# A graph layer's message sums: 128 single rows and 24 gathered chunks per block in place of 96 and 28, with row offsets computed on VectorE

## The chip, the core and the metric

The kernel runs on one core of a Trainium2 chip. The metric is the device time of one launch in microseconds. Before the change, three runs took 15717.78, 15709.04 and 15708.98 us, a median of 15709.04.

In the profile PE is TensorE, DVE VectorE, ACT ScalarE, POOL GpSimd and SP SyncE. ACT and SP can issue DMAs too; their queues are written ACTq and SPq. L234 is line 234 of the kernel.

## The reference, cut to what matters

There are 50,000 nodes with 128 features and 1,650,000 edges, sorted by destination. Each edge has one of two types.

```python
Xs = X[src]
m_data = Xs @ W_data.T + b_data
m_ctrl = Xs @ W_control.T + b_control
msg = jnp.where((edge_types == 0)[:, None], m_data, m_ctrl)
agg = jax.ops.segment_sum(msg, dst, num_segments=X.shape[0])
h = x + jax.nn.relu(agg + (X @ W_self.T + b_self))
out = (h - mean(h)) / sqrt(var(h) + 1e-5)      # over the 128 features
```

So the row `X[src]` has to be fetched for every edge, and rows are summed by destination and type. The weights can be applied to the sums instead of to every edge.

## The kernel before

**Blocks and chunks.** The edges are cut into blocks of `BE = C * CH + X` = 28 * 128 + 96 = 3680 edges; there are 449 blocks, and ten of them (`GB`) make a group. A block has 28 chunks of 128 edges and one more "chunk" of 96. A block's work goes in `Q` = 4 steps of `R` = 7 chunks; the 96 extra edges belong to the fourth step.

**Two ways to fetch rows.** The rows of a 128-edge chunk come with one indirect DMA issued by POOL (L246), which reads 128 node numbers from a tile and gathers 128 rows of 512 bytes into a tile `y`. `y` has 70 buffers. The rows of the 96 extra edges come one by one, into the tile `yx`: SP and ACT issue 48 plain DMAs of 512 bytes each (L234). For that, the engine loads 12 node numbers into registers with one instruction (L229), once per step, which I call a turn; the DMA's address is the register times the row's length.

**Sums.** DVE makes a one-hot matrix per chunk (L198), which tells for each edge its destination within a window of `W` = 36 nodes and its type. PE multiplies the fetched rows with it (L249), so a step's sums by destination and type stand in PSUM (`acc`, four buffers). DVE counts edges by destination (L208, L213), and PE spreads the counts over rows (L252). DVE then adds a step's `acc` to the block's sums (`add`, L260) at a place that it loads into a register.

**Windows.** A block's destinations lie in a window of `B` = 128 nodes; sums run in a ring of three tiles. ACT copies the part of the last block's sums that the next window shares (`take_over`, L263 and L265). PE applies the weights (`layer`, L270 to L273), DVE makes h and its moments (L278 to L282), ACT takes the root (L284), DVE scales (`store`, L290 and L292), and SP stores the block (L293). SP also loads the windows of x and of its transpose (L187, L189).

**Order.** The order of the instructions on each engine is written out by hand, by the loop at the end of `straight`. In iteration b there stand, in this order: the windows of block b + 3; in every tenth iteration the loads of the next group's edges (`load_edges`, L95 and L99, in SP's queue); the last `add` of block b - 1 and the `take_over`; then for each step q the products of block b, with `layer`, `add`, `moments`, the one-hot of block b + 2, `store` and `counts` among them, and a turn of single rows for block b + 2 on SP and on ACT. On ACT a block is thus: copy, root, four turns of rows. On SP it is: two window loads, a turn of rows, a store, three turns of rows.

Of the kernel before, what the change touches and what calls it, by code (L numbers as in the profile page):

```python
# [11 lines left out]
F32 = mybir.dt.float32  # L12
BF16 = mybir.dt.bfloat16
I32 = mybir.dt.int32
AF = mybir.ActivationFunctionType
ALU = mybir.AluOpType
AX = mybir.AxisListType
# [3 lines left out]

N = 50000
D = 128
E = 1650000
P = 128
EPS = 1e-5
# [2 lines left out]
DST_PAD = 65536  # L29


R = 7
W = 36
Q = 4
B = 128
C = R * Q
X = 96
C1 = C + 1
BE = C * CH + X
NBLK = -(-E // BE)  # L40
REST = E - (NBLK - 1) * BE
RCH = -(-REST // CH)
LAST = REST - (RCH - 1) * CH
assert RCH <= C
GB = 10
# [5 lines left out]
U = 35  # L51
CPP = -(-(-(-E // CH) + U) // P)
NCH = CPP * P
# [11 lines left out]
def row_bcast(ap, n=P):  # L65
    return bass.AP(tensor=ap.tensor, offset=ap.offset, ap=[[0, n], *ap.ap])


def straight(ctx, tc, c, x, x_t, src_t, dst_t, etype_t, src_x, dst_first, out):
# [10 lines left out]
    nc = tc.nc  # L80
    keep = ctx.enter_context(tc.tile_pool(name="keep", bufs=1))
    keep_ps = ctx.enter_context(tc.tile_pool(name="keep_ps", bufs=1, space=bass.MemoryType.PSUM))
    eds = ctx.enter_context(tc.tile_pool(name="eds", bufs=2))
# [3 lines left out]
    ps = ctx.enter_context(tc.tile_pool(name="ps", bufs=4, space=bass.MemoryType.PSUM))  # L87
    ps_o = ctx.enter_context(tc.tile_pool(name="ps_o", bufs=2, space=bass.MemoryType.PSUM))

    idx_g, d_g, t_g, one_g, col_g = {}, {}, {}, {}, {}  # L90
    stats = keep.tile([P, 2, GROUPS], F32, name="stats")

    def load_edges(g):
        t = eds.tile([1, GB * X], I32, name="one_g")
        nc.sync.dma_start(t, src_x[None, g * GB * X:(g + 1) * GB * X])  # L95
        one_g[g] = t
        for name, a, of in (("idx_g", src_t, idx_g), ("d_g", dst_t, d_g), ("t_g", etype_t, t_g)):
            t = eds.tile([P, GC], I32, name=name)
            nc.sync.dma_start(t, a[:, g * GC:(g + 1) * GC])  # L99
            of[g] = t  # L100


    load_edges(0)
    BL = TBL
    first_i = keep.tile([P, BL, Q], I32, name="first_i")
    nc.sync.dma_start(first_i.rearrange("p b q -> p (b q)"), row_bcast(dst_first))
    base = keep.tile([P, BL, 1], F32, name="base")
    nc.vector.tensor_scalar(base, first_i[:, :, 0:1], 0.0, float(N - B), op0=ALU.max, op1=ALU.min)
    nc.vector.memset(base[:, 0:1, :], 0.0)
    nc.vector.memset(base[:, NBLK - 1:, :], float(N - B))  # L110
    begin = keep.tile([P, BL, Q], F32, name="begin")
    nc.vector.tensor_tensor(begin, first_i, base.to_broadcast([P, BL, Q]), op=ALU.subtract)
    nc.vector.tensor_scalar(begin, begin, 0.0, float(B - W), op0=ALU.max, op1=ALU.min)
    place_i = keep.tile([1, BL, Q], I32, name="place_i")
    nc.vector.tensor_copy(place_i, begin[0:1, :, :])
    nc.vector.tensor_tensor(begin, begin, base.to_broadcast([P, BL, Q]), op=ALU.add)
    base_i = keep.tile([1, BL], I32, name="base_i")
    nc.vector.tensor_copy(base_i, base[0:1, :, 0])
    shift = keep.tile([1, NBLK], F32, name="shift")
    nc.vector.memset(shift, 0.0)  # L120
    nc.vector.tensor_tensor(shift[:, 1:], base[0:1, 1:NBLK, 0], base[0:1, :NBLK - 1, 0], op=ALU.subtract)
    shift_i = keep.tile([1, NBLK], I32, name="shift_i")
    nc.vector.tensor_scalar(shift_i, shift, 0.0, float(B), op0=ALU.max, op1=ALU.min)


    num = keep.tile([P, 2 * W], F32, name="num")
    nc.gpsimd.iota(num, pattern=[[1, 2 * W]], base=0, channel_multiplier=0,
                   allow_small_or_imprecise_dtypes=True)
    num_ps = keep_ps.tile([P, 2 * W], F32, name="num_ps")
    nc.vector.tensor_copy(num_ps, num)  # L130
# [3 lines left out]
    for t in range(2):  # L134
        nc.vector.memset(to_row[:, t, t:t + 1], 1.0)
    bias = keep.tile([3, D], F32, name="bias")
    for i, b in enumerate((c["b_data"], c["b_ctrl"], c["b_self"])):
# [4 lines left out]
    RING = 3  # L142
    sums = [keep.tile([P, 3, 2 * B], F32, name=f"sums{i}") for i in range(RING)]
    for t in sums:
# [4 lines left out]
    def columns(g):  # L149
# [4 lines left out]
        rel_b, d_b = (a.rearrange("p (b c) -> p b c", c=C1) for a in (rel, d))  # L154
        nc.vector.tensor_tensor(rel_b[:, :, :C].rearrange("p b (q r) -> p b q r", r=R),
                                d_b[:, :, :C].rearrange("p b (q r) -> p b q r", r=R),
                                first[:, :, :, None].to_broadcast([P, GB, Q, R]), op=ALU.subtract)
        nc.vector.tensor_tensor(rel_b[:, :, C:], d_b[:, :, C:], first[:, :, Q - 1:], op=ALU.subtract)
        col = eds.tile([P, GC], F32, name="col_g")
        nc.vector.tensor_scalar(col, t, 0.0, float(W), op0=ALU.not_equal, op1=ALU.mult)  # L160
        nc.vector.tensor_tensor(col, col, rel, op=ALU.add)
        chk = eds.tile([P, GC], F32, name="chk")
        nc.vector.scalar_tensor_tensor(chk, d, float(DST_PAD), rel, op0=ALU.is_lt, op1=ALU.mult)
        nc.vector.tensor_reduce(stats[:, 0, g:g + 1], chk, AX.X, ALU.min)
        nc.vector.tensor_reduce(stats[:, 1, g:g + 1], chk, AX.X, ALU.max)
        col_g[g] = col

    def chunks_of(b, q):

        n = C1 if b < NBLK - 1 else RCH if b < NBLK else 0  # L170
        return range(q * R, max(q * R, min((q + 1) * R if q < Q - 1 else C1, n)))

    def steps_of(b):
        return [q for q in range(Q) if len(chunks_of(b, q))]
# [3 lines left out]
    ohs, cnts, ys, accs, xws, xTs, pos, hs, mvs, sds = {}, {}, {}, {}, {}, {}, {}, {}, {}, {}  # L178

    def base_of(b):  # L180
        return nc.values_load(base_i[0:1, b:b + 1], engines=[SP], min_val=0, max_val=N - B,
                              skip_runtime_bounds_check_because="it was clamped to this")

    def window(b):
        at = base_of(b)
        xw = stp.tile([B, D], F32, name="xw", bufs=5)
        nc.sync.dma_start(xw, x[bass.ds(at, B), :])  # L187
# [4 lines left out]
    def onehot(b):  # L192
# [3 lines left out]
        n = C1 if b < NBLK - 1 else RCH  # L196
        oh = ohp.tile([P, C1, 2 * W], F32, name="oh")
        nc.vector.tensor_tensor(oh[:, :n, :], col_g[g][:, i * C1:i * C1 + n, None].to_broadcast([P, n, 2 * W]),  # L198
# [3 lines left out]
    def counts(b):  # L202

        cnt = ohp.tile([P, Q, 2 * W], BF16, name="cnt")
        with nc.allow_low_precision(reason="whole numbers up to R + 1"):
            whole = [q for q in range(Q) if len(chunks_of(b, q)) == R]
            n = len(whole)
            nc.vector.tensor_reduce(cnt[:, :n, :], ohs[b][:, :n * R, :].rearrange("p (q r) w -> p q w r", r=R),  # L208
                                    AX.X, ALU.add)
            for q in steps_of(b):  # L210
# [5 lines left out]

    SHARE = X // 2
    TURN = SHARE // Q
    RANGE = dict(min_val=0, max_val=N - 1, skip_runtime_bounds_check_because="a node's number")

    def single_rows(b, q):

        if q == 0:
            ys[b] = stp.tile([X, D], F32, name="yx", bufs=AHEAD + 2)
        g, i = divmod(b, GB)
        both = []
        for j, (eng, dma) in enumerate(((SP, nc.sync), (ACT, nc.scalar))):
            at = j * SHARE + q * TURN
            _, nodes = nc.values_load_multi_w_load_instructions(  # L229
                one_g[g][0:1, i * X + at:i * X + at + TURN], engines=[eng], **RANGE)  # L230
            both.append([(dma, at + k, node) for k, node in enumerate(nodes)])
        for pair in zip(*both):
            for dma, row, node in pair:
                dma.dma_start(ys[b][row:row + 1, :], x[bass.ds(node, 1), :])  # L234

    def products(b, q):
        g, i = divmod(b, GB)
# [2 lines left out]
        for k in ks:  # L240
            if k == C:
                r, y = X, ys.pop(b)
            else:
                r = LAST if b == NBLK - 1 and k == RCH - 1 else P
                y = gat.tile([P, D], F32, name="y")
                nc.gpsimd.indirect_dma_start(  # L246
# [20 lines left out]
    def layer(b):  # L267
        a = sums[b % RING]
        po = ps_o.tile([B, D], F32, name="po")
        nc.tensor.matmul(po, xTs.pop(b), c["wselfT"], start=True, stop=False)  # L270
        nc.tensor.matmul(po, a[0:3, 2, :B], bias, start=False, stop=False)  # L271
        for t in range(2):
            nc.tensor.matmul(po, a[:, t, :B], c["wmsgT"][:, t * D:(t + 1) * D], start=False, stop=t == 1)  # L273
        pos[b] = po

    def moments(b):
# [6 lines left out]
        sd = stp.tile([B, 1], F32, name="sd")  # L283
        nc.scalar.activation(sd, mv[:, 1:2], AF.Sqrt, bias=c["eps"][:B, :])  # L284
        hs[b], mvs[b], sds[b] = h, mv, sd
# [9 lines left out]
    with tc.manual_schedule():  # L295
# [5 lines left out]
        for b in range(AHEAD):  # L301
            for q in range(Q):
                single_rows(b, q)
        for b in range(NBLK + 1):
            if b + 3 < NBLK:
                window(b + 3)
            g, i = divmod(b, GB)
# [41 lines left out]
    both = keep.tile([2, 1], F32, name="both")  # L349
# [9 lines left out]
def general(ctx, tc, c, x, src, dst, etype, out):  # L359
# [166 lines left out]
    with tc.For_i(0, BGROUPS, 1) as g:  # L526
# [43 lines left out]
        sd = grp.tile([NB, G], F32, name="sd")  # L570
        nc.scalar.activation(sd, mv[:, :, 1], AF.Sqrt, bias=eps[:NB, :])
        rstd = grp.tile([NB, G], F32, name="rstd")
# [8 lines left out]
def gnn_resnorm(  # L581
# [46 lines left out]
    with ExitStack() as own:  # L628
        straight(own, tc, c, x, x_t, src_t, dst_t, etype_t, src_x, dst_first, out)
# [38 lines left out]
```

## Time and profile before

| what | value |
|---|---|
| median of the runs | 15709.04 us |
| the profiled execution's own time | 15709.39 us |
| its span in the profile | 15707.6 us |
| busy: PE, DVE, ACT, POOL | 62%, 24%, 2%, 76% |
| granted TensorE clock | 1.00 |
| DMA queue of POOL: packets, MB | 401760, 823.58 |
| DMA queue of SP (q1): packets, MB | 256650, 120.61 |
| DMA queue of ACT (q10): packets, MB | 43446, 11.29 |

The busy share counts what an engine computes. Register steps, waits and the issuing of DMAs aren't in it, so an engine that issues DMAs all the time can stand there as idle. A group's line gives its count, its busy time, the mean of one, and behind the second bar the idle time before it with who ended most of it. In a timeline each line is a start, a length, the engine (with q for its queue), the source line, the operation and how many were merged. In a line's own view the three numbers in the middle are the shortest, median and longest duration in ns, and then come the first and the last start in the window.

All 40 slices of the span look alike: the kernel is one steady loop of 449 blocks, some 35 us each.

### The profile page before, as it was taken

What the parts mean: (1) busy time and instruction counts of PE and PEld (TensorE: products, weight loads), DVE (VectorE), ACT (ScalarE), POOL (GpSimd) and SP (SyncE); (2) the same over time, 40 slices, a digit from 0 to 9 for tenths busy, and PEclk for the clock granted to TensorE, in tenths of its full rate; (3) what the DMA queues carried; (4) which work ended last, traced back from release to release, by engine and by line L of the source; (5) the groups of instructions that cost most, each with busy time, mean ns of one, the idle gap of its engine ahead of it and who ended that gap; (6) DMA issues with size and microseconds to landing.
All of it is one profiled execution on the core that took longest, in us unless ns stands there. A gap on an engine that the chain in (4) does not pass through costs nothing.

```text
span 15707.6 us, 248219 instructions
## 1 busy us (share of the span) xinstructions
PE 9719.2 (62%) x33193; PEld 7477.1 (48%) x33194; DVE 3846.6 (24%) x5740; ACT 365.0 (2%) x903; POOL 11860.3 (76%) x12563
## 2 busy tenths in 40 slices
PE   5666666666666666666666666666666666666666
PEld 4444444444444444444444444444444444444444
DVE  3222222222222222222222222222222222222222
ACT  0000000000000000000000000000000000000000
POOL 7777777777777777777777777777777777777777
DMA  2222222222222222222222222222222222222222
GB/s 65 62 62 62 62 63 62 62 62 62 62 62 62 63 62 62 62 62 62 62 62 63 62 62 62 62 62 62 62 63 62 62 62 62 62 62 62 63 62 58
DMA packets 703530, 971.47 MB, mean 62 GB/s; under 512 B 267712, under 2 KB 500803, under 8 KB 701856
## 3 DMA queue, kind: packets, MB, share of 16 engines
q0 software_dynamic: 401760, 823.58, 20.1%
q1 hardware_dynamic: 256650, 120.61, 2.9%
q10 hardware_dynamic: 43446, 11.29, 0.3%
q14 instruction: 1397, 11.44, 0.2%
q8 instruction: 277, 4.54, 0.1%
HBM read 924.99 MB, written 29.43 MB: 61 GB/s over the span
## 4 chain that ended last, share of the span: by engine, by line
DMA 39%; issue 37%; PE 14%; POOL 8%; ACTq 2%; DVE 0%; SPq 0%; POOLq 0%; ACT 0%; DVEq 0%
DMA y<-in_x,idx_g 38%; PE acc L249 9%; POOL y L246 8%; PE po L273 2%; PE po L271 1%; DMA yx<-in_x 1%; PE po L270 1%; ACTq L234 1%; ACTq L229 0%; PE acc L252 0%; SPq L234 0%; POOLq L246 0%; SPq L229 0%; DVE sums L260 0%; DVE st L280 0%
## 5 line engine op out<-in xcount | busy, mean ns | idle before, releaser
L246 POOL DMA_INDIRECT y<-in_x,idx_g x12555 | 11859.4, 945 | 3832.3 <-issue 2666.4
L249 PE MATMUL acc<-oh,y 128*128 128x72 f32 x25110 | 8397.3, 448 | 5957.2 <-DMA y<-in_x,idx_g 5852.6
L249 PEld LDWEIGHTS acc<-oh,y 128*128 128x128 f32 x25110 | 6240.9, 314 | 7996.6 <-DMA y<-in_x,idx_g 7247.8
L260 DVE TENSOR_TENSOR sums<-acc,sums 128x108 f32 x1794 | 486.0, 271 | 10835.0 <-PE acc L252 9773.4
L208 DVE TENSOR_REDUCE cnt<-oh 128x216 bf16<-128x1512 f32 (+1 forms) x449 | 1268.5, 2825 | 0.1
L198 DVE TENSOR_TENSOR oh<-col_g,num_ps 128x2088 f32<-128x2088 f32 (+1 forms) x449 | 1030.7, 2296 | 0.0
L252 PEld LDWEIGHTS <-to_row 128*128 128x128 bf16 x3588 | 654.4, 198 | 0.0
L273 PE MATMUL po<-wmsgT,sums 128*128 128x128 f32 x1796 | 548.7, 461 | 0.0
L213 DVE TENSOR_REDUCE cnt<-oh 128x72 bf16<-128x576 f32 (+1 forms) x449 | 526.1, 1172 | 0.0
L265 ACT COPY sums<-sums 128x384 f32 x448 | 229.4, 512 | 11662.5 <-DMA yx<-in_x 11590.1
L252 PE MATMUL acc<-cnt,to_row 128*128 128x36 bf16 x3588 | 480.1, 217 | 0.0
L273 PEld LDWEIGHTS po<-wmsgT,sums 128*128 128x128 f32 x1796 | 416.3, 322 | 100.7 <-issue 100.7
L278 DVE SCALAR_TENSOR_TENSOR h<-po,xw 128x128 f32<-128x128 f32 x449 | 130.8, 291 | 949.2 <-PE po L273 949.2
L271 PE MATMUL po<-bias,sums 3*128 3x128 f32 x898 | 355.6, 497 | 9.5 <-DVE sums L260 8.2
L270 PE MATMUL po<-wselfT,xT 128*128 128x128 f32 x898 | 348.7, 492 | 0.0
L249 PE MATMUL acc<-oh,yx 96*128 96x72 f32 x896 | 284.6, 421 | 7.6 <-DMA yx<-in_x 7.6
L271 PEld LDWEIGHTS po<-bias,sums 3*128 3x128 f32 x898 | 223.3, 308 | 110.1 <-issue 110.1
L249 PEld LDWEIGHTS acc<-oh,yx 96*128 96x128 f32 x896 | 235.6, 323 | 7.8 <-DMA yx<-in_x 7.8
L270 PEld LDWEIGHTS po<-wselfT,xT 128*128 128x128 f32 x898 | 228.9, 317 | 0.0
L284 ACT ACTIVATE sd<-mv,eps 128x1 f32<-128x1 f32 x449 | 132.2, 295 | 3667.7 <-DVE mv L282 3667.7
L292 DVE TENSOR_SCALAR o<-h,mv,rstd 128x128 f32<-128x128 f32 x449 | 155.9, 347 | 16.6
L280 DVE BATCH_NORM_STATS2 st<-h 128x6 f32<-128x128 f32 x449 | 132.3, 295 | 15.3
(61 smaller groups left out, 294.9 us busy)
## 6 DMA issues: line engine op xcount, KB each, us to landing
yx<-in_x ACTq DMA_DIRECT2D x21504, 0.5 KB
yx<-in_x SPq DMA_DIRECT2D x21504, 0.5 KB
y<-in_x,idx_g POOLq DMA_INDIRECT x12555
xw<-in_x SPq DMA_DIRECT2D x449, 64.0 KB
xT<-in_x_t SPq DMA_DIRECT2D x449, 64.0 KB
out<-o SPq DMA_DIRECT2D x449, 64.0 KB
idx_g<-in_src_t SPq DMA_DIRECT2D x45, 145.0 KB
d_g<-in_dst_t SPq DMA_DIRECT2D x45, 145.0 KB
```

Of the source, the lines that this page charges most:

```text
L198: nc.vector.tensor_tensor(oh[:, :n, :], col_g[g][:, i * C1:i * C1 + n, None].to_broadcast([P, n, 2 * W]), num_ps[:, None, :].to_broadcast( ...
L208: nc.vector.tensor_reduce(cnt[:, :n, :], ohs[b][:, :n * R, :].rearrange("p (q r) w -> p q w r", r=R), AX.X, ALU.add)
L213: nc.vector.tensor_reduce(cnt[:, q, :], ohs[b][:, k[0]:k[-1] + 1, :].rearrange("p r w -> p w r"), AX.X, ALU.add)
L234: dma.dma_start(ys[b][row:row + 1, :], x[bass.ds(node, 1), :])
L246: nc.gpsimd.indirect_dma_start(out=y[:r], out_offset=None, in_=x, in_offset=bass.IndirectOffsetOnAxis(ap=idx_g[g][:r, i * C1 + k:i * C1 + ...
L249: nc.tensor.matmul(acc[:, :2, :].rearrange("p t w -> p (t w)"), y[:r], ohs[b][:r, k, :], start=k == ks[0], stop=k == ks[-1])
L252: nc.tensor.matmul(acc[:, 2, :], to_row[:, t, :], cnts[b][:, q, t * W:(t + 1) * W], start=t == 0, stop=t == 1)
L260: nc.vector.tensor_tensor(part, accs.pop((b, q)), part, op=ALU.add)
L265: nc.scalar.copy(sums[b % RING][:, :, :B], sums[(b - 1) % RING][:, :, bass.ds(at, B)])
L270: nc.tensor.matmul(po, xTs.pop(b), c["wselfT"], start=True, stop=False)
L271: nc.tensor.matmul(po, a[0:3, 2, :B], bias, start=False, stop=False)
L273: nc.tensor.matmul(po, a[:, t, :B], c["wmsgT"][:, t * D:(t + 1) * D], start=False, stop=t == 1)
```

## The change

A block becomes 24 chunks and 128 single edges: `R` goes from 7 to 6, `X` from 96 to 128, `BE` from 3680 to 3200, and the number of blocks from 449 to 516. The windows shrink with it: `W` from 36 to 34, `B` from 128 to 112. A turn is 16 rows per queue instead of 12.

The registers hold byte offsets instead of node numbers. After a group's node numbers are loaded, DVE multiplies them all by the 512 bytes of a row (a tile `at_g` of one partition); SP and ACT load their registers from that tile. x and the target tile are viewed as bytes, so that the address of a row is the register itself.

```diff
+U8 = mybir.dt.uint8
...
+ROW = 4 * D
...
-R = 7
-W = 36
+R = 6
+W = 34
 Q = 4
-B = 128
+B = 112
 C = R * Q
-X = 96
+X = 128
...
-    idx_g, d_g, t_g, one_g, col_g = {}, {}, {}, {}, {}
+    idx_g, d_g, t_g, at_g, col_g = {}, {}, {}, {}, {}
...
     def load_edges(g):
         t = eds.tile([1, GB * X], I32, name="one_g")
         nc.sync.dma_start(t, src_x[None, g * GB * X:(g + 1) * GB * X])
-        one_g[g] = t
+        at = eds.tile([1, GB * X], I32, name="at_g")
+        nc.vector.tensor_scalar(at, t, float(ROW), None, op0=ALU.mult)
+        at_g[g] = at
...
-    RANGE = dict(min_val=0, max_val=N - 1, skip_runtime_bounds_check_because="a node's number")
+    RANGE = dict(min_val=0, max_val=(N - 1) * ROW, skip_runtime_bounds_check_because="where a node's row is")
+    x_bytes = x.rearrange("n d -> (n d)").bitcast(U8)[None, :]
...
-            _, nodes = nc.values_load_multi_w_load_instructions(
-                one_g[g][0:1, i * X + at:i * X + at + TURN], engines=[eng], **RANGE)
-            both.append([(dma, at + k, node) for k, node in enumerate(nodes)])
+            _, rows = nc.values_load_multi_w_load_instructions(
+                at_g[g][0:1, i * X + at:i * X + at + TURN], engines=[eng], **RANGE)
+            both.append([(dma, at + k, row) for k, row in enumerate(rows)])
         for pair in zip(*both):
-            for dma, row, node in pair:
-                dma.dma_start(ys[b][row:row + 1, :], x[bass.ds(node, 1), :])
+            for dma, k, row in pair:
+                dma.dma_start(ys[b][k:k + 1, :].bitcast(U8), x_bytes[:, bass.ds(row, ROW)])
```

## The prediction

> **What bounds the kernel now.** I read the page first, then the timelines of POOL, ACT and SP over one block, then the row line L234 by itself.
>
> ```profile
> span 15707.6 us, 248219 instructions
> ...
> L246 POOL DMA_INDIRECT y<-in_x,idx_g x12555 | 11859.4, 945 | 3832.3 <-issue 2666.4
> ...
> L265 ACT COPY sums<-sums 128x384 f32 x448 | 229.4, 512 | 11662.5 <-DMA yx<-in_x 11590.1
> ...
> yx<-in_x ACTq DMA_DIRECT2D x21504, 0.5 KB
> yx<-in_x SPq DMA_DIRECT2D x21504, 0.5 KB
> ```
>
> POOL's timeline shows one gather after another, 0.94 us busy and 0.30 us of issue, with no other wait; the first starts at 3.91 us, the last at 15692.27. That is 15688.36 / 12554 = 1.2497 us each, so 28 gathers are 34.99 us, and 449 blocks of 28 (the last has 11) are the span. POOL is the bound. The reader's question is how much room SP and ACT, which issue the single rows, have left in 34.99 us. ACT's timeline over one block, then SP's:
>
> ```profile
> 8023.78 0.51 ACT L265 COPY sums<-sums 128x384 f32 x1 [25.28 <-DMA yx<-in_x]
> 8033.34 0.29 ACT L284 ACTIVATE sd<-mv,eps 128x1 f32<-128x1 f32 x1 [9.05 <-DVE mv L282]
> 8034.39 24.32 ACTq L234 DMA_DIRECT2D yx<-in_x  x48
> 8059.50 0.51 ACT L265 COPY sums<-sums 128x384 f32 x1 [25.86 <-DMA yx<-in_x]
> ```
> ```profile
> 8026.41 4.82 SPq L234 DMA_DIRECT2D yx<-in_x  x12
> 8032.08 0.38 SPq L293 DMA_DIRECT2D out<-o  x1
> 8039.62 19.43 SPq L234 DMA_DIRECT2D yx<-in_x  x36
> ```
>
> ACT is "2% busy", but its queue issues rows for 24.3 us plus four register loads, and its only real slack is the 9.05 us in which it waits for DVE's moments, which come only when POOL's gathers have come. SP waits about 6 us before its second turn. Now one row:
>
> ```profile
> L234 ACTq DMA_DIRECT2D yx<-in_x x143: 227/228/468, 7999.9 to 8093.2; - x143
> L234 ACTq FUSED_REGOPS  x142: 37/37/37, 8000.1 to 8093.0; - x142
> L234 ACTq MOVE yx<-in_x x142: 29/29/29, 8000.2 to 8093.1; - x142
> ```
> ```profile
> L234 ACTq DMA_DIRECT2D yx<-in_x x11: 227/228/249, 8047.8 to 8052.1; - x11
> ```
>
> With the gaps between them (28, 29 and 40 ns in the trace) the three steps make 391 ns from row to row. But the second fence, eleven rows of one turn while SP issues too, takes 4.3 us for ten steps: 0.43. The missing 0.04 is waiting. In the trace each queue's rows take turns on four semaphores (on ACT 102, 104, 106, 109, then 102 again), and a row starts no sooner than some 20 ns after the row four before it has landed. The trace's landing records give 1.38 us from issue to landing where the other queue issues nothing within 1 us, and 1.65 where it issues four; by the paces of rows 5 to 11 of a turn (0.436 mean over the run) four rows take 1.70 to 1.74. **So where both queues issue, rows already go by landing, not by issue.**
>
> **The change, part by part.**
>
> Gathers: 515 blocks of 24 and a last one of 16 make 12376; at 1.2497 they take 15466 us, with 3.9 before and 14.4 behind 15484. POOL's period per block becomes 29.99 us. This is the gain of the change, 1.4%, if the rest keeps up.
>
> Register step: 37 ns and its gap of 29 go, so ACT's issue step is 391 - 66 = 325 ns. It helps only rows that don't wait.
>
> Rows: 64 per queue and block instead of 48, in four turns of 16. One turn on ACT, both queues issuing: from the register load's start to the first row 1.26 us now (load 1.06), less 0.066, plus four more values. A load of one value (L263) is 0.56 and of twelve 1.06, 0.045 each, so +0.18: 1.37. Row 4 starts 0.63 + 0.40 + 0.40 behind row 1 now, 1.235 with the step gone thrice. Rows 5 to 16 are three rounds of one landing. I take 1.70 (measured pace times four), so 5.10; the last issue is 0.23. Sum 7.93. The same sum for today's 12 rows gives 5.05 from first row to last end, where the trace's mean is 5.12. Four turns: 31.7 us, already over 29.99.
>
> Between two blocks' rows ACT must read its shift and copy the sums (rows end 8058.71, copy 8059.50: 0.79), then wait for DVE. What this takes when gathers are not late is seen at the kernel's start, where rows of three blocks go out first and DVE waits for ACT:
>
> ```profile
> 94.92 0.27 DVE L260 TENSOR_TENSOR sums<-acc,sums 128x108 f32 x1 [38.40 <-ACT sums L265]
> 95.11 0.28 DVE L278 SCALAR_TENSOR_TENSOR h<-po,xw 128x128 f32<-128x128 f32 x1
> ...
> 95.75 0.18 DVE L282 BATCH_NORM_AGGREGATE mv<-st 128x2 f32<-128x6 f32 x1
> ```
>
> ACT's copy starts at 94.38 and mv ends at 95.93: 1.55. With 0.03 to the next load, 2.4 us per block. Hence 34.1 us per block, ACT (and SP, which has 64 rows, three larger DMAs and their loads, about 34) sets the end, and POOL waits for buffers once its 70 tiles are filled: that is what is late next.
>
> The new DVE product (L95's load, then 1280 values on one partition): not in the trace. 2088 values a partition take 2.30 us on DVE, so 1.4 by its elements; a 128x1 operation takes 0.15. In DVE's order it stands ahead of the last add of the block before, and waits for a load in SP's queue. Queued behind it are that add, ACT's copy, all of ACT's rows, and PE after four sums. Bounds: nothing, if SP is early; at most SP's lag. SP stores at 8032.08 the o that DVE made at 8004.23 (L292), so SP runs a block behind: the load would go out some 39 us after DVE wants it, and land about 1 to 3 later, so 40 us at worst, 51 times, 2040 us. I take the nearest row, a load that someone waits for: idx_g is issued at 1.19 and POOL starts at 3.91, 2.7; with the product 4.1, times 51 groups, 209 us. The lag can't be paid each time, since SP and ACT meet at each turn's semaphores.
>
> W 34, B 112, 516 blocks for 449: PE per block 24 pairs of 0.70, yx 0.7, counts 1.1, layer 2.6, 21 us; DVE's two large steps go from 2.30 to 1.87 and 4.0 to 3.3 us; windows and stores of 56 KB for 64. All of it lies beside 34 us of rows, so I cost it at nothing; without that cover PE's 21 is still under POOL's 29.99.
>
> Sum: start 29 (ACT's first rows follow its first load at 29.1) + 515 x 31.7 = 16325 + 513 x 2.4 = 1231 + tail 60 (gathers of the last blocks are done, PE has three blocks of about 20) + 209 = **17,850 us**. The profiled execution took 15709.39 for a span of 15707.6, the median 15709.04, so no correction: +13.6%.
>
> The Trainium skill ("DMA: Bandwidth & Descriptors", section "Anatomy of one DMA", for the software path) holds that a DMA costs about 2.0 us fixed, mostly the receipt of the write, which speaks against many small rows. Rounds of 2.0 by that page would make a turn 8.83 and the sum 19,700; the landings here are 1.38 to 1.74 on SP's and ACT's queues, so the measurement decides.
>
> **Bounds of the landing.** Below: 1.40, as with one queue alone, gives a turn of 7.03, blocks of 28.1 + 2.4, and 515 x 28.1 + 1231 + 89 = 15,790. Above: it grows from two queues to fuller ones as it did from one to two (1.65 / 1.38 = 1.2), 2.0: turn 8.83, 35.3 a block, 515 x 35.3 + 1231 + 89 + 209 = 19,710.
>
> **Rivals.**
> 1. *Faster: POOL stays the bound*, 15,484 us. It decides once four turns and 2.4 fit in 29.99, so a turn of 6.90, which needs landings of at most 1.36 us with both queues busy. For it: the trace has landings of 1.2, and issue alone would make 16 rows 5.3 us, a turn of 6.7. Against it: 1.38 is the mean even alone, 1.65 together, and four rows in flight stay four. Chance 0.12.
> 2. *Landing as if alone*, 15,790 to 16,600. For it: ACT's first turn runs against a waiting SP today. Against it: with 64 rows each, neither has idle time left. 0.08.
> 3. *DVE waits out SP's lag each group*: 17,645 + 2040 = 19,690. For it SP's store, a block late; against it that ACT then idles while SP catches up, so the lag must form anew. 0.08.
> 4. *The byte form does not do what it says*: a register step stays, or a row's issue gets longer. With the step left in, rows still go by landing; four turns gain 4 x 0.26 us, 545 us over 515 blocks, 18,400. 0.05.
>
> **How the numbers follow.** The forecast has 0.64, rivals 0.12, 0.08, 0.08, 0.05, and 0.03 lies within 0.2% of today (about what a measurement of this kernel can tell from no change), where landings come out at 1.36 to 1.39. The forecast's own range is 16,600 to 19,200. The range of 8 in 10 leaves out rival 1 and takes in both bounds: 15,790 to 19,710. Slower 0.85, same 0.03, faster 0.12.
>
> **What would show it.** Right: POOL's gathers wait for PE (buffers) and their spacing in the mean is near 1.43; ACT's wait at L284 shrinks from 9 to about 1 us; DVE's adds wait for ACT's copy; no FUSED_REGOPS on the row line, but ten row steps late in a turn still take 4.2 us or more; a block of ACT's rows takes over 30 us. Wrong: ten steps in 3.3 us, POOL's idle at 0.30 throughout, and ACT still waiting several us at L284.

## The result and the profile after

The changed kernel takes 17145.63 us (median of 4 runs, 17093.68 to 17207.41) beside 15709.01 for the kernel before: ratio 1.0915, 95% interval 1.0866 to 1.0963. The forecast was 17,850 in a range of 15,790 to 19,710. The profiled execution took 17093.68 us for a span of 17091.8. Line numbers moved by four to six: gather L251, single rows L239, their register load L234, ACT's copy L270, the root L289, the product L99, the store L298.

From the page of the changed kernel (count, busy, mean, then the idle time ahead and who ended it):

```profile
span 17091.8 us, 256316 instructions
...
L251 POOL DMA_INDIRECT y<-in_x,idx_g x12376 | 11688.1, 944 | 5329.7 <-PE acc L254 2288.0
...
L265 DVE TENSOR_TENSOR sums<-acc,sums 128x102 f32 x2063 | 534.8, 259 | 11896.0 <-ACT sums L270 11739.8
...
L289 ACT ACTIVATE sd<-mv,eps 112x1 f32<-112x1 f32 x516 | 152.0, 295 | 629.1 <-DVE mv L287 622.5
...
yx<-in_x ACTq DMA_DIRECT2D x32960, 0.5 KB
```

POOL, which had no wait but its own issue before, now waits for PE to free its tiles: its first gather starts at 3.72 us and its last at 17018.48, a mean spacing of 1.375 us for 1.2497. DVE waits for ACT's copy, 11,740 us in all, and ACT's wait at the root fell from 3,668 us to 629. ACT, 2% busy, is the bound. Its timeline, then SP's:

```profile
8028.50 0.47 ACT L270 COPY sums<-sums 128x336 f32 x1 [31.35 <-DMA yx<-in_x]
8030.05 0.30 ACT L289 ACTIVATE sd<-mv,eps 112x1 f32<-112x1 f32 x1 [1.07 <-DVE mv L287]
8031.26 29.29 ACTq L239 DMA_DIRECT2D yx<-in_x  x64
8061.34 0.47 ACT L270 COPY sums<-sums 128x336 f32 x1 [31.00 <-DMA yx<-in_x]
```
```profile
8028.63 5.52 SPq L239 DMA_DIRECT2D yx<-in_x  x16
8035.63 0.34 SPq L298 DMA_DIRECT2D out<-o  x1
8037.14 21.83 SPq L239 DMA_DIRECT2D yx<-in_x  x48
8059.74 0.32 SPq L191 DMA_DIRECT2D xw<-in_x  x1
```

From copy to copy 32.84 us pass here. From the first register load of one block to that of the next it is 33.08 in the mean: four turns of 7.27, 7.69, 7.64 and 7.65, together 30.25, 0.10 between them, and 2.73 between the last row of one block and the first load of the next. That last gap is 2.36 us in nine blocks of ten, and some 5.9 in the tenth, where DVE waits for the load of the next group's node numbers. 514 periods from copy to copy, 32.98 each, with 115.6 ahead of the first copy and 25.8 behind the last make up the whole span. SP's first turn starts at 8028.63, 2.6 us ahead of ACT's.

The row line by itself shows that the register step is gone (no FUSED_REGOPS), and a row is 29 + 228 ns and two gaps:

```profile
L239 ACTq MOVE yx<-in_x x194: 29/29/29, 8000.0 to 8099.9; - x194
L239 ACTq DMA_DIRECT2D yx<-in_x x194: 227/228/501, 8000.6 to 8100.0; - x194
```

One thing is needed to read five of the runs below: e1 to e4 ran on a chip on which the kernel before itself takes 22,970 us, and e12 on one on which it takes 23,258, so their times can't be compared with those of the rest.

### The profile page after: what moved, and what is told of

Read it like the earlier page. It is cut to its first block, busy times and chain, and to the rows that moved or that the text cites. A ratio compares the mean times of both kernels' runs of the same rounds, so it can differ in the third digit from the quotient of the medians.

```text
span 17091.8 us, 256316 instructions
## 1 busy us (share of the span) xinstructions
PE 7041.1 (41%) x34043; PEld 6711.1 (39%) x34044; DVE 3742.3 (22%) x6646; ACT 398.6 (2%) x1037; POOL 11689.0 (68%) x12384
## 4 chain that ended last, share of the span: by engine, by line
DMA 46%; ACTq 32%; issue 9%; PE 8%; SPq 3%; ACT 1%; DVE 1%; DVEq 0%; POOL 0%
DMA yx<-in_x 43%; ACTq L239 22%; ACTq L234 10%; PE acc L254 7%; SPq L239 1%; ACT sums L270 1%; DMA xT<-in_x_t 1%; DVE sums L265 1%; ACTq L268 1%; DMA xw<-in_x 1%; DMA one_g<-in_src_x 0%; SPq L234 0%; DMA out<-o 0%; PE po L278 0%; PE po L276 0%
## 5 line engine op out<-in xcount | busy, mean ns | idle before, releaser
L251 POOL DMA_INDIRECT y<-in_x,idx_g x12376 | 11688.1, 944 | 5329.7 <-PE acc L254 2288.0
L254 PE MATMUL acc<-oh,y 128*128 128x68 f32 x24752 | 5617.8, 422 | 6941.7 <-DVE sums L265 6879.9
L254 PEld LDWEIGHTS acc<-oh,y 128*128 128x128 f32 x24752 | 5461.8, 330 | 6993.3 <-DVE sums L265 6931.0
L265 DVE TENSOR_TENSOR sums<-acc,sums 128x102 f32 x2063 | 534.8, 259 | 11896.0 <-ACT sums L270 11739.8
L212 DVE TENSOR_REDUCE cnt<-oh 128x204 bf16<-128x1224 f32 x516 | 1198.9, 2323 | 0.1
L202 DVE TENSOR_TENSOR oh<-col_g,num_ps 128x1700 f32<-128x1700 f32 x516 | 977.1, 1894 | 0.0
L270 ACT COPY sums<-sums 128x336 f32 x515 | 243.2, 472 | 16045.1 <-DMA yx<-in_x 7708.6
L278 PE MATMUL po<-wmsgT,sums 128*112 128x128 f32 x2064 | 616.8, 455 | 0.0
L257 PE MATMUL acc<-cnt,to_row 128*128 128x34 bf16 x4126 | 547.8, 214 | 0.0
L217 DVE TENSOR_REDUCE cnt<-oh 128x68 bf16<-128x476 f32 x516 | 514.2, 997 | 0.0
L278 PEld LDWEIGHTS po<-wmsgT,sums 128*112 128x112 f32 x2064 | 451.2, 297 | 128.9 <-issue 128.9
L275 PE MATMUL po<-wselfT,xT 128*112 128x128 f32 x1032 | 385.4, 477 | 0.0
L99 DVE TENSOR_SCALAR at_g<-one_g 1x1280 int32<-1x1280 int32 x52 | 42.4, 815 | 1300.8 <-DMA one_g<-in_src_x 1300.8
L289 ACT ACTIVATE sd<-mv,eps 112x1 f32<-112x1 f32 x516 | 152.0, 295 | 629.1 <-DVE mv L287 622.5
```

Source lines behind the costliest of these rows:

```text
L217: nc.vector.tensor_reduce(cnt[:, q, :], ohs[b][:, k[0]:k[-1] + 1, :].rearrange("p r w -> p w r"), AX.X, ALU.add)
L251: nc.gpsimd.indirect_dma_start(out=y[:r], out_offset=None, in_=x, in_offset=bass.IndirectOffsetOnAxis(ap=idx_g[g][:r, i * C1 + k:i * C1 + ...
L254: nc.tensor.matmul(acc[:, :2, :].rearrange("p t w -> p (t w)"), y[:r], ohs[b][:r, k, :], start=k == ks[0], stop=k == ks[-1])
L257: nc.tensor.matmul(acc[:, 2, :], to_row[:, t, :], cnts[b][:, q, t * W:(t + 1) * W], start=t == 0, stop=t == 1)
L265: nc.vector.tensor_tensor(part, accs.pop((b, q)), part, op=ALU.add)
```

## The experiments

The theory that I went in with: rows go by landing, four in flight on each queue; a turn of 16 takes about 7.6 us; and when four turns and the chain between blocks exceed POOL's 24 x 1.2497 = 29.99 us, they set the time. The rivals are that it is the smaller block (516 in place of 449, each with windows, sums and a store), the byte form of the address, or DVE's new wait.

| run | what it is | us | ratio to before, interval |
|---|---|---|---|
| after | the change | 17145.63 | 1.0915, 1.0866 to 1.0963 |
| e10 | with 96 rows | 15656.98 | 0.9967, 0.9953 to 0.9981 |
| e5 | with 28 chunks, product late | 15594.59 | 0.9926, 0.9912 to 0.994 |
| e6 | without byte offsets and product | 18539.78 | 1.1799, 1.1782 to 1.1816 |
| e11 | byte offsets alone | 15718.01 | 1.0006, 0.9992 to 1.002 |
| e7 | ACT's rows alone | 16400.53 | one run |
| e8 | product late | 17918.92 | 1.1407, 1.139 to 1.1423 |
| e9 | 112 rows, product late | 18519.8 | 1.179, 1.1773 to 1.1807 |
| e1 | as e6, other chip | 27732.56 | 1.2078, 1.2058 to 1.2098 |
| e2 | as e10, other chip | 21330.75 | 0.929, 0.9275 to 0.9306 |
| e3 | 28 chunks, 128 rows, other chip | 22751.96 | 0.9906, 0.9889 to 0.9922 |
| e4 | as e7, other chip | 20817.6 | one run |
| e12 | product late, wait kept, other chip | 24845.39 | 1.0678, 1.066 to 1.0695 |

**Rows or smaller blocks: e10, e2.**

```diff
-X = 128
+X = 96
```

> The changed kernel with 96 single rows in place of 128 (24 chunks, byte offsets, the product where the change has it). Landing theory: turns of 12 rows take some 6.0 us, four and 2.5 us are 26.6, under POOL's 29.99; 12501 gathers x 1.2497 + 18 = 15,641, ratio 0.9957. If DVE's wait for the product's load is now paid, as it is the one long wait left (26 us at most, 53 groups), up to 17,000. Rival (the block's shape sets the time): 521 x 33 = 17,200.

```profile
L251 POOL DMA_INDIRECT y<-in_x,idx_g x12501 | 11814.8, 945 | 3817.4 <-issue 2612.6
...
L289 ACT ACTIVATE sd<-mv,eps 112x1 f32<-112x1 f32 x521 | 153.6, 295 | 2234.7 <-DVE mv L287 2216.4
```

15,657 beside an expected 15,641. These are e10's lines: POOL's idle is its own issue again, 0.31 us a gather (3817.4 / 12501), and ACT waits for DVE at the root, 4.3 us a block. 521 of the smaller blocks cost nothing that shows. So the loss of the change comes with the 32 more rows. e2 is the same kernel:

> The changed kernel with 96 single rows per block instead of 128 (blocks of 3168 edges, 521 of them, 12501 gathers), all else as changed. Row theory (the rows of ACT and SP set the block): turns of 12 rows take about 5.85, a block's rows and copy 25.9 us, under the 29.99 of 24 gathers, so POOL is the bound: 12501 x 1.2497 + 18 = 15,640 us. Rival (what slows is what comes with each smaller block, the windows, the sums' chain and the wait for the product on DVE): blocks stay near 33 us, 521 of them, 17,200.

On its chip ACT's rows go at 0.70 us a step (0.40 in e10), so it can't check the numbers of the theory.

**As many rows in larger blocks: e5, e3.** e5 keeps 28 chunks with 128 rows, and moves DVE's product two blocks behind its load (e3 leaves the product where the change has it).

```diff
-R = 6
-W = 34
+R = 7
+W = 36
...
-B = 112
+B = 128
...
+            if i == GB // 2 + 2 and g + 1 < GROUPS:
+                offsets(g + 1)
```

> 28 chunks and 128 single rows per block (windows 36 and 128), byte offsets, and the product on DVE moved two blocks behind its load, so that DVE has nothing to wait for. Row theory: rows and copy take 32.8 us, POOL's 28 gathers 34.99, so POOL is the bound: 12447 gathers x 1.2497 + 18 = 15,573 us, 0.87% under before. Rival (single rows at 64 per queue slow the kernel whatever POOL's share is, through DMA contention or DVE's chain): 445 blocks at over 36 us, above 16,000.

> The changed kernel with the 28 chunks (windows 36 and 128) of before, and 128 single rows: 445 blocks, 12447 gathers. Row theory: rows and copy still take 30.2 + 2.6 = 32.8 us, but POOL's block is 34.99, so POOL is the bound: 12447 x 1.2497 + 18 = 15,573 us, 0.87% under before. Rival (DVE's wait for the load of the node numbers, behind SP's lag, stops the sums once per group): up to 40 us x 44, at most 17,300; anything over 15,650 would speak for it.

```profile
L255 POOL DMA_INDIRECT y<-in_x,idx_g x12447 | 11774.7, 946 | 3800.9 <-issue 2433.2
...
L293 ACT ACTIVATE sd<-mv,eps 128x1 f32<-128x1 f32 x445 | 131.0, 294 | 491.7 <-DVE mv L291 491.7
```

In e5, 15,594.59, POOL is the bound again and the kernel is 0.7% faster than before, the best of all. It is a narrow fit: ACT's wait at the root is 1.1 us a block (491.7 / 445), for its four turns of 8.15 us and 2.3 fill 34.9 of the 34.99 us that 28 gathers take: ACT is as good as full too. The time by the number of gathers, 12447 x 1.2497 + 18 = 15,573, was met within 0.2%. The same 128 rows that cost 9% beside 24 chunks (14% with the product late, e8) cost nothing beside 28.

**The byte form: e6, e1, e11.** e6 is the changed kernel with node numbers in the registers and no product; e11 is the kernel before with the byte form as its one change.

```diff
-                at_g[g][0:1, i * X + at:i * X + at + TURN], engines=[eng], **RANGE)
+                one_g[g][0:1, i * X + at:i * X + at + TURN], engines=[eng], **RANGE)
...
-                dma.dma_start(ys[b][k:k + 1, :].bitcast(U8), x_bytes[:, bass.ds(row, ROW)])
+                dma.dma_start(ys[b][row:row + 1, :], x[bass.ds(node, 1), :])
```

> The changed kernel's blocks (24 chunks, 128 single rows) with the register step per row and without the product on DVE, as in the first run of this form. Landing theory: the step's 66 ns hide mostly in the wait for the landing of the row four before; a turn goes from 7.56 to about 8.3 us, a block from 33.0 to 35.5, 18,400 us. Rival 1 (rows go by their own steps): 4.2 us more per block, 37.2, 19,260. Rival 2 (the offsets bring nothing): 17,150 or less.

> The changed kernel's blocks (24 chunks, 128 single rows, windows of 112) with the addressing of before: node numbers in the registers, a register step per row, no product on DVE. Landing theory (with four rows in flight per queue a row waits for the landing of the row four before it): most of the 66 ns is hidden in that wait, a turn goes from 7.56 to about 8.3 us, a block from 33.0 to 35.5, 18,400 us. Rival 1 (rows go by their own issue steps, so each step saved is time saved): 64 x 0.066 = 4.2 us more per block, 37.2, 19,260. Rival 2 (the byte offsets bring nothing in this state): 17,150 less what the product on DVE cost.

> The kernel before (28 chunks, 96 rows, its windows) with byte offsets made on DVE as its one change. Landing theory: POOL's 12555 gathers x 1.2497 + 18 = 15,709 stand, and the rows' 66 ns are gained beside them: 15,700 to 15,720, ratio 0.999 to 1.001. ACT's wait at the root grows from 9 us to about 12. If DVE's wait for the product's load is paid in each of 45 groups (26 us less what 70 buffers cover), up to 16,880.

e6 took 18,540, e11 15,718. The byte form does what it says, and it is worth much only where rows are the bound. e11's wait at the root stayed at 8.0 us a block (3589.1 / 448) where 12 was expected: in its second turn the first rows stand for up to 1.5 us each, beside SP's store, and the gain went there.

**Four in flight: e7, e4.** SP issues no rows, so 64 edges of each block are left out of the sums.

```diff
-        for j, (eng, dma) in enumerate(((SP, nc.sync), (ACT, nc.scalar))):
-            at = j * SHARE + q * TURN
+        for eng, dma in ((ACT, nc.scalar),):
+            at = q * TURN
...
-                r, y = X, ys.pop(b)
+                r, y = SHARE, ys.pop(b)
```

> The changed kernel without SP's half of the single rows (64 edges per block left out of the sums), as in the first run of this form; eight semaphores go round among ACT's rows. Landing theory: ten row steps take 3.3 us although landings stay at 1.2 us or more, a turn is about 6.5, POOL is the bound at about 15,484. Rival (never more than four under way, or a slower pace set elsewhere): ten steps take 3.5 us or more and the turn over 6.9.

> The changed kernel without SP's half of the single rows: ACT issues its 64, and 64 edges of each block are left out of the sums. All eight semaphores then go round among ACT's rows, so eight are in flight. Landing theory: rows no longer wait, ten row steps take 3.3 us although landings stay at 1.3 us or more (over four rows in flight), a turn is about 6.5, a block 28.5 and POOL is the bound at 15,484. Rival (a queue can't have more than four under way, whatever the semaphores, or the pace is set by the machinery that moves them): row steps stay over 0.35, ten take 3.5 us or more.

ACT's timeline in e7, then SP's:

```profile
8009.41 0.47 ACT L270 COPY sums<-sums 128x336 f32 x1 [29.65 <-DMA yx<-in_x]
8010.96 0.29 ACT L289 ACTIVATE sd<-mv,eps 112x1 f32<-112x1 f32 x1 [1.07 <-DVE mv L287]
8012.16 27.99 ACTq L239 DMA_DIRECT2D yx<-in_x  x64
8040.95 0.47 ACT L270 COPY sums<-sums 128x336 f32 x1 [29.70 <-DMA yx<-in_x]
```
```profile
8013.47 0.34 SPq L298 DMA_DIRECT2D out<-o  x1
8014.31 0.32 SPq L191 DMA_DIRECT2D xw<-in_x  x1
8014.85 0.35 SPq L193 DMA_DIRECT2D xT<-in_x_t  x1
```

Three of ACT's four turns take 6.86 us, a row each 0.330, the issue step; the first takes 8.72. The block came to 31.65 us, not to POOL's 29.99. The trace says why, and corrects "four". It records which semaphore each DMA signals and waits for. There are eight, and the DMAs of *both* queues take turns on them; a DMA waits until the one before it on its semaphore has landed. Four per queue is only what comes out when the two queues take strictly alternate turns. With ACT alone 85% of its rows wait for the row eight before them, which has landed by then. And where a semaphore went to one of SP's large transfers, ACT's next row on it waits for that transfer. In the block shown the store takes semaphore 105, and its last part lands at 8015.20; ACT's next row on 105 (the sixth of its first turn) starts at 8015.22. The window of L191 takes 106, lands at 8016.20, and ACT's row on 106 starts at 8016.22. So e7 took away two things at once, the other queue's traffic (landing 1.40 us in the mean) and the limit of four, and it doesn't tell their parts.

**DVE's wait: e8, e12.** e8 is the changed kernel with the product two blocks behind its load, so that DVE doesn't wait for the load.

```diff
-        at = eds.tile([1, GB * X], I32, name="at_g")
-        nc.vector.tensor_scalar(at, t, float(ROW), None, op0=ALU.mult)
-        at_g[g] = at
+        one_g[g] = t
...
+            if i == GB // 2 + 2 and g + 1 < GROUPS:
+                offsets(g + 1)
```

> The changed kernel, with DVE's product of a group's node numbers moved from just behind its load to two blocks later, so that DVE no longer waits for that load. Landing theory: DVE waits for ACT's copy in every block anyhow (25 us at the group's product in the trace, as in any block), so the time stays within 0.6% of the changed kernel's 17,146: 17,050 to 17,150, and the block stays 32.8 to 33.1 us. The step of 209 us in the prediction would give 16,940. Rival 3 (DVE waits out SP's lag in each group, 26 us in the trace, 51 times, 1300 us): about 15,850.

17,919, 4.5% *slower* than the change: every expectation failed. Two things changed at once, and the trace tells them apart. The gap between blocks is 2.36 us in every block now, with no 5.9 in the tenth, so moving the product gained 190 us (the gaps of the whole run are 1,209 us in e8 and 1,399 in the change). But the turns grew by 1,003 us in all, in the mean of the whole run from 7.57 to 8.06 us each. With 15 us more at the end these make the 828 us between the two profiled executions; the medians are 773 apart. The lists of waits (engine, tile and line, what was waited for: us in all, times, longest), of the changed kernel and of e8:

```profile
PE acc L254 <- DVE sums L265: 6879.9, 460, 19.6
...
DVE at_g L99 <- DMA one_g<-in_src_x: 1300.8, 52, 39.4
...
PE acc L254 <- DMA yx<-in_x: 34.8, 2, 18.1
```
```profile
DVE sums L269 <- ACT sums L274: 13998.2, 514, 51.5
PE acc L258 <- DMA yx<-in_x: 8615.2, 500, 20.1
```

Without DVE's wait PE stands for the single rows in 500 of 516 blocks. Counted by register loads, SP's turns of a block start 34 us after ACT's in e8: SP works a whole block behind. In the changed kernel DVE waits for a load in SP's queue once in ten blocks, and the lag isn't there: SP's turns start 2.8, 1.4, 1.9 and 2.2 us *ahead* of ACT's of the same block. And ACT's turns are longer in e8, from 4,000 us on 8.08 us beside 7.56. The rows of one turn, the changed kernel's ACT from 8034.1 to 8037.0 and e8's from 8034.0 to 8038.6:

```profile
L239 ACTq DMA_DIRECT2D yx<-in_x x9: 227/228/228, 8034.2 to 8036.9; - x9
```
```profile
L243 ACTq DMA_DIRECT2D yx<-in_x x11: 227/228/241, 8034.4 to 8038.4; - x11
```

Nine rows at 0.33 us each beside eleven at 0.40. The semaphores tell them apart. Of ACT's rows (the first two of a turn left out, from about 4,000 us on), by how many of ACT's rows back ACT last used the semaphore, the share and the mean step to the row:

| kernel | four back | more than four | mean step | landing, mean |
|---|---|---|---|---|
| before | 83%, 426 ns | 17%, 398 ns | 422 ns | 1.55 us |
| changed | 54%, 424 ns | 45%, 334 ns | 383 ns | 1.55 us |
| e8 | 88%, 431 ns | 12%, 341 ns | 420 ns | 1.65 us |
| e6 | 88%, 432 ns | 12%, 408 ns | 429 ns | 1.59 us |

A row in a round of four costs the same in the changed kernel and in e8, 424 and 431 ns, and 4 x 0.424 is the 1.70 of the prediction. The others go near the issue step, 0.33 us without the register step and 0.39 with it. What differs is mainly their share: with e8's shares the changed kernel's steps would make 0.88 x 424 + 0.12 x 334 = 413 ns, so by this estimate 30 of the 37 ns between the two are the dealing out of semaphores and 7 the steps themselves. Fifteen steps of 37 ns are 0.55 us, and a turn differs by 0.52. Which semaphore a row takes is written into the program: e2 and e10, one program on two chips, have the same sequence in all 24,960 of ACT's rows. In all kernels with both queues in which DVE waits at the load, 34 to 65% of ACT's rows go in fours; in all others, the kernel before among them, 83 to 88%.

Is it the lag itself that makes the turns longer? e8's own start speaks against it. There the lag grows slowly. In blocks 46 to 57 (1,580 to 1,980 us) SP is already 29 to 31 us behind, but only 32 to 54% of ACT's rows go in fours, and a turn takes 7.64 us. From block 58 on the lag is 34 us and more, 88% go in fours, and a turn takes some 8.05 us. The share is not all, though: in blocks 22 to 27 only 20% go in fours, and a turn takes 7.86.

e12 puts the wait back, and nothing else: DVE multiplies one value of the load, into a tile that nobody reads.

```diff
         one_g[g] = t
+        seen = eds.tile([1, 1], I32, name="seen")
+        nc.vector.tensor_scalar(seen, t[:, 0:1], float(ROW), None, op0=ALU.mult)
```

> As e8_late_product (the product two blocks behind its load), and one more: where the load stands, DVE multiplies one value of it into a tile that nobody reads, so DVE again waits for SP's load once in ten blocks, and does nothing else for it. Theory after e8_late_product (the wait is what counts: it keeps SP from lagging a block behind ACT, SP's rows then start 1 to 4 us ahead of ACT's, and rows land in 1.53 us instead of 1.67): 17,150 (17,090 to 17,220), SP's turns 2 to 3 us ahead of ACT's of the same block. Rival (the wait does nothing, and it is the place of the product, or when its tile is ready, that made the changed kernel faster than e8_late_product): 17,920, SP's turns some 34 us behind ACT's.

Its time, on another chip, tells nothing about 17,150 or 17,920. Its trace tells of the order: DVE waits, and the lag is gone. A line of DVE's timeline and one of the page:

```profile
8078.43 0.14 DVE L100 TENSOR_SCALAR seen<-one_g 1x1 int32<-1x1 int32 x1 [29.28 <-DMA one_g<-in_src_x]
```
```profile
L260 PE MATMUL acc<-oh,yx 128*128 128x68 f32 x1030 | 327.0, 419 | 113.7 <-DMA yx<-in_x 103.2
```

PE's wait for rows is 114 us (8,615 in e8), SP's first turns start 1.9 us ahead of ACT's (in e1, with no such wait and on such a chip, 54 us behind), and 65% of ACT's rows go in fours, between the change and e8. With the steps of the changed kernel that would be 0.65 x 424 + 0.35 x 334 = 393 ns, a turn of 7.7. Against e8's 8.06 that is some 720 us less over the run, and the wait takes 190 back, so by that estimate some 530 of the 773 us. So the wait by itself changes both the lag and the dealing out. How it comes to change the dealing out isn't shown, and that the time follows on a chip like that of e8 was not measured.

**The edge: e9.** e8 with `X = 112`, a turn of 14 rows.

> 24 chunks as in the changed kernel, but 112 single rows for 128, a turn of 14 rows per queue; product moved as in e8_late_product. Landing theory: a turn of 16 rows takes 7.56 us in the changed kernel's trace; two rows less at 0.33 to 0.38 each and 0.1 of register load make 6.7 to 6.8, four turns and 2.5 us 29.3 to 29.7 a block, just under POOL's 24 x 1.2497 = 29.99. So POOL is the bound again: 12438 gathers x 1.2497 + 18 = 15,562 (15,560 to 15,700), ratio to before 0.991 to 0.999. If the rows' part of a block is larger than that by 1 us, the 519 blocks go at 30.7: 15,950. Rival (the shape of the block, 519 smaller blocks with their windows and sums, sets the time, not the rows): 519 x 33 = 17,100.

18,520, a clear miss: fewer rows than e8, and slower. The register load by itself (shortest, median, longest ns), in e9 and then in the changed kernel:

```profile
L238 ACTq TENSOR_LOAD <-at_g x11: 1237/1547/3371, 8001.6 to 8092.1; - x11
L238 SPq TENSOR_LOAD <-at_g x11: 1172/1439/3138, 8002.1 to 8093.8; - x11
```
```profile
L234 SPq TENSOR_LOAD <-at_g x12: 976/1134/1317, 8002.9 to 8094.0; - x12
L234 ACTq TENSOR_LOAD <-at_g x12: 1022/1294/1346, 8004.5 to 8096.1; - x12
```

In this stretch loading 14 values takes up to 3.4 us, 16 values at most 1.35. On both queues the second and the fourth turn of a block pay it (3.38 and 3.30 on ACT), the first and third less (1.24 and 1.51). Why 14 is so dear was not settled. Two loads of some 2.0 us too much are 4 of e9's 35.58 us a block; without them it would be some 31.6, still over 29.99, because 86% of the rows go in fours here too.

## Why the prediction was right, and where it was not

**What held.** POOL stops being the bound; four turns and a chain between blocks set the end. The profile shows it as announced: DVE's adds wait for ACT's copy (514 times), the root's wait is 1.07 us, the register step is gone, POOL waits for PE. Smaller blocks cost nothing beside that (e10). The issue step is 0.33 us (e7), and a round of four rows is 1.70, as taken. Four marks were near misses: POOL's mean spacing 1.375 for 1.43, the last ten row steps of a turn 3.8 us in the mean for 4.2, a block of ACT's rows 29.2 for over 30, the product 0.82 us for 1.4.

**The step that failed is "rows 5 to 16 are three rounds of one landing"**, which rests on "four rows in flight stay four". Four is no property of a queue but of how eight shared semaphores are dealt out, and in the changed program 45% of ACT's rows are free of it: a turn is 7.56 us and not 7.93. The prediction measured the right pace and held the wrong thing fixed. Where the program leaves 88% in fours, e8, its sum without the product, 17,645, is 1.5% under the 17,919 measured. So the direction and the bound were foreseen for the right reason, while the distance of 4% depends on a dealing out that the prediction didn't consider.

**The price of DVE's product held**, 4.1 us in each of 51 groups, 209 us. DVE waits for the load 25 us each time, and most of that it would have waited for ACT's copy anyhow. But the end of the wait comes too late. ACT's timeline and DVE's at one group:

```profile
3209.54 27.89 ACTq L239 DMA_DIRECT2D yx<-in_x  x64
3240.44 0.47 ACT L270 COPY sums<-sums 128x336 f32 x1 [31.82 <-DMA idx_g<-in_src_t]
3243.26 0.29 ACT L289 ACTIVATE sd<-mv,eps 112x1 f32<-112x1 f32 x1 [2.35 <-DVE mv L287]
```
```profile
3239.37 0.82 DVE L99 TENSOR_SCALAR at_g<-one_g 1x1280 int32<-1x1280 int32 x1 [25.32 <-DMA one_g<-in_src_x]
3240.11 0.24 DVE L265 TENSOR_TENSOR sums<-acc,sums 128x102 f32 x1
3240.95 0.26 DVE L265 TENSOR_TENSOR sums<-acc,sums 128x102 f32 x1 [0.59 <-ACT sums L270]
```

ACT's rows end at 3237.43, and its copy, which needs DVE's add behind the product, starts 3.01 us later; in the block at 8031 it starts 0.79 later. With the root's wait of 2.35 in place of 1.07 that is 3.5 us. (The turns ahead of such a gap take 28.9 us in sum for the 30.4 of other blocks; why is open.) Over the run 51 of the 514 gaps between blocks are longer than 2.36 us, by 192 us together, and in e8 none is. Moving the product away still cost 773 us, for the turns grew. The lag of SP, "must form anew", was seen; that a wait which forbids it also changes the rotation was not, and the trace of before could not show it.

**From forecast to measurement:**

| term | forecast, us | trace, us |
|---|---|---|
| start, up to the first register load of a row | 29 | 5 |
| 515 x 4 turns, with the 0.03 us between them | 16,325 | 15,645 |
| chain between blocks, 2.4 and 2.36 each | 1,231 | 1,207 |
| product | 209 | 192 |
| tail | 60 | 43 |
| sum | 17,854 | 17,092 |

The median lies 54 us over the profiled span. So 680 of the 704 us by which the forecast was too high are the turns; the other terms and that 54 nearly cancel. The first row of the forecast is misread: the load at 29.1 us in the trace of before is that of ACT's third turn, and the first stands at 2.2. That nearly came out even by luck, since ACT's first two turns are slow, 30 us together in the changed kernel, and stand in the second row here.

**The rivals.** POOL as the bound needed turns of 6.90; 6.86 came only with ACT alone (e7). Landing as if alone, 1.40, was not seen with both queues. DVE paying SP's whole lag in each group, 40 us: it paid 3.5 to 3.8, for with the wait no lag forms. The register step left in: e6, 18,540; of the 1,394 us between it and the change 621 are the step (e6 to e8; the prediction's 4 x 0.26 us gives 545) and 773 came with the product's wait, its own price taken off.

The Trainium skill ("DMA: Bandwidth & Descriptors", section "Anatomy of one DMA") gives about 2.0 us fixed for a DMA of the software path; on SP's and ACT's queues rows landed in 1.40 us (e7) to 1.68 us (e5) in the mean, and the sum by 2.0, 19,700, an estimate, would have been further off.

## What to carry to other kernels

An engine that only issues small DMAs has no idle time that "2% busy" shows: its room is turns times pace, and here 128 rows fitted under 28 gathers and not under 24. Where the pace is set by rows in flight, read from the trace which semaphores the rows take, for that rotation belongs to the program and another order of the same work deals it out anew. Before you move a wait off the path, ask what else it orders: here the wait cost 190 us, and without it the kernel was 4.5% slower.

## What the runs showed of the hardware

- A register load of 14 values took 1.2 to 3.6 us, one of 12 values 0.75 to 1.3 and one of 16 values 0.97 to 1.5 (turns of e9, e10 and the change).
- Rows on one queue land the later the more the other queue has just issued: 1.44, 1.47, 1.61 and 1.61 us on ACT's queue in the change with none, one, two and three of SP's rows in the microsecond before, and 1.43, 1.50, 1.65 and 1.73 in e8.
- On the chips of e1 to e4 and e12, ACT and SP stop, mostly for 0.6 to 0.7 us, between the issue of one row and the next register step, which waits for nothing, in 6 to 8% of the rows on ACT and 13 to 18% on SP (e1, e2, e12). On the other chips 0.8% of the rows show a stop, of 0.31 to 0.36 us. Why is open.
